# A graph layer on one Trainium2 core: the first norm of a joining group in six pieces, and a new order of passes in the FFN stream

## The chip, the core and the metric

The program runs on one core of one Trainium2 chip. The core has five engines that each follow their own list of instructions and meet only at semaphores: TensorE (PE in the profile, with its weight loads shown apart as PEld), VectorE (DVE), ScalarE (ACT), GpSimd (POOL) and SyncE (SP), which here only starts transfers. The metric is the device time of one execution in microseconds (us); lower is better.

## The reference, cut to what matters

A graph layer over 12500 nodes with 256 channels and 200000 edges sorted by destination:

```python
xn = layernorm(x)
support = xn @ gnn_weight                                  # 12500 x 256
agg = segment_sum(support[src] * edge_weight[:, None], dst, 12500)
x = x + relu(agg) + linear_attention(xn)                   # 4 heads of 64
h = layernorm(x)
for _ in range(30):                                        # the FFN
    h = h + 0.01 * tanh(h)
    h = h * sigmoid(h)
    h = layernorm(h, ln_w, ln_b)
    h = einsum("bsc,dc->bsd", h, W) + b
out = x + h
```

All is in float32. The 30 iterations on 12500 rows are the bulk of the work. A row never meets another row inside the FFN, so the rows can be worked in any order.

## The kernel before

**Tiling.** The 12500 nodes are 98 tiles of 128 rows. Four tiles make a group (G = 4), so there are 24 full groups and a last one of two tiles. One FFN iteration on one group is a *pass*; there are 25 x 30 = 750.

**Three stages.** First, x is loaded, normed and written out (`xnd`), the edge lists are transposed, and a part of the attention's key and value products is made. Second, the rest of these products, followed by the *mix chain*: a short row of dependent small matrices (`py`, `y`, `pbd`, `bd`, `pm`, `at`, `pm`, `mix`, lines 837 to 873) that folds the attention into one 256 x 256 matrix `mix`. Between its links the function `another_quad` is called twice. Third, the *FFN stream*, from about line 1025 to the end, in which all else is done step by step.

**The quads.** Edges are gathered 128 at a time: an indirect DMA issued by GpSimd (`gathers`, L196) brings the rows of `xnd` that belong to 128 edges into a tile `xg`, of which there are 16. Four of these make a *quad*: `selections` makes a matrix of weights on VectorE (L222, L227, L235), `sum_quad` multiplies on TensorE (L248, tile `pq`), ScalarE copies the sums of two quads (`copy_quads`, L259), and `add_quads` adds them by another matmul (L273) to a ring of nodes `pa`, which is copied out and cleared in `free_nodes` (L287, L288). There are 391 quads, about 16 to a group. Once a group's quads are done, its W matrix (aggregate times `wg`) can run, and with its mix matrix (`xnT` times `mix`) it makes the group's `base`, the x that goes into the FFN.

**The stream.** `plan()` writes out, before any instruction is issued, a list of steps. A step has at most one item: a pass, a mix matrix or a W matrix. It may also have a quad, a number of gathers, and the start of a group. `plan` keeps a clock of its own from fixed costs (T_PASS = 4.4 and so on) and takes a quad when the modelled landing of its gathers (T_LAND after the issue) lies in the past. At most ABREAST = 5 groups are in their 30 passes at a time, and two passes of one group are at least APART = 4 steps apart. Which of the ready groups gets the step is decided by

```python
if len(started) < len(groups) - 2 * ABREAST:
    g = min(ready, key=lambda g: (active[g][0], g))               # longest since its last pass
else:
    g = min(ready, key=lambda g: (active[g][1], active[g][0]))    # fewest passes done
```

A group starts ("joins") in the very step in which another one has left, if its base is there.

**A pass over several steps.** With its item in step k, a group is transposed on TensorE (L1001, tile `pt`) and copied by ScalarE (L1008, tile `zT`) in step k, multiplied by the FFN's matrix in k + 1 (L1014, tile `po`), and in k + 2 goes through tanh (ACT L960), the sum (DVE L966), silu (ACT L967), the statistics (DVE L973, `stats`) and their power of -1/2 on GpSimd (L977, L979). `normed` (DVE L987, tile `z`) follows one step later, and the group is ready to be transposed again. After its 30th pass, `po` is added to `base` into a tile `z` (L1075), and SyncE sends that to memory (L91). There are three `z` buffers, which `normed`, the outputs and the first norms share.

**A join before the change.** In step k, at its end: `ln_stats` with four bn_stats, four bn_aggr and a tensor_scalar on VectorE (L119, L121, L123) and a power on GpSimd (L125). In k + 1: the shift (L1097), four norms, half on VectorE (L1102) and half on ScalarE (L1107), and tanh. In k + 2: `act2`. In k + 3: `stats`. The group's first pass is planned for k + 5 or later.

Each engine works in the order in which the instructions were issued. GpSimd therefore does gathers and powers in one row, and a power that waits for VectorE holds back the gathers behind it.

Of the kernel before, what the change touches and what calls it, by code (L numbers as in the profile page):

```python
# [30 lines left out]
def gps_layer(  # L31
# [78 lines left out]
    nc.vector.memset(eps_t, EPS)  # L110
    root = first.tile([P, 1], F32, name="root")
    nc.scalar.activation(root, eps_t, AF.Sqrt)

    def ln_stats(pool, tl, nt, name):

        st = pool.tile([P, G, 6], F32, name=name + "_st")
        mv = pool.tile([P, G, 2], F32, name=name + "_mv")
        for j in range(nt):
            nc.vector.bn_stats(st[:, j, :], tl[:, j, :])  # L119
        for j in range(nt):  # L120
            nc.vector.bn_aggr(mv[:, j, :], st[:, j, :])  # L121
        ve = pool.tile([P, G], F32, name=name + "_ve")
        nc.vector.tensor_scalar(ve[:, :nt], mv[:, :nt, 1], 1.0, EPS, ALU.mult, ALU.add)  # L123
        rs = pool.tile([P, G], F32, name=name + "_rs")
        nc.gpsimd.tensor_tensor(rs[:, :nt], ve[:, :nt], mhalf[:, :nt], ALU.pow)  # L125
        return mv, rs

    def transposes_of(nat):

# [597 lines left out]
    with ExitStack() as ph:  # L727
# [112 lines left out]
        py = p_kv.tile([D + 1, HEADS, P], F32, name="pkv")  # L840
        for hd in range(HEADS):
            nc.tensor.matmul(py[:, hd, :], lhsT=psum_kv[:, hd, :], rhs=lk[:, hd % (P // D), :], start=True, stop=True)
        y = w1.tile([D + 1, HEADS, P], F32, name="y")
        nc.vector.tensor_copy(y, py)
        another_quad()
# [3 lines left out]
        for hd in range(HEADS):  # L849
            r = slice(hd % (P // D) * D, (hd % (P // D) + 1) * D)  # L850
            nc.vector.tensor_scalar(bd[r, hd // (P // D), r], pbd[r, hd, :], 1.0 / N, None, ALU.mult)


        at = w1.tile([P, KC, C], F32, name="at")
# [10 lines left out]
        for m in range(KC):  # L865
            for h in range(KC):
                nc.tensor.matmul(
                    pm[:, m, :], lhsT=at[:, h, m * P : (m + 1) * P], rhs=woT[:, h, :],
                    start=(h == 0), stop=(h == KC - 1),
                )  # L870
        nc.vector.scalar_tensor_tensor(
            mix, bo_r[:, None, :].to_broadcast([P, KC, C]), 1.0 / C, pm, op0=ALU.mult, op1=ALU.add
        )
# [6 lines left out]


    def plan():
        T_PASS, T_MATRIX, T_QUAD, T_GATHER, T_LAND, T_POW, T_STATS, T_CHAIN = 4.4, 3.5, 1.2, 1.25, 3.0, 1.3, 4.4, 14.0
        now, pool = 0.0, 4.0
        quads, got, started = ed.summed, ed.gathered, []
        whole, based = [], {}
        active, mixed, steps, k = {}, 0, [], 0
        landed = {t: 0.0 for t in range(got)}
        summed, passes = 0, 0
        pows = {}  # L890
        while len(based) < len(groups) or active or len(started) < len(groups):
            item, nq, cost, start = None, 0, 0.0, None
            octets = NO if quads == NQ else quads // 2
            while summed < len(groups) and octets > last_of[min((summed + 1) * G, NT) * P // SLOT - 1]:
                whole.append(summed)
                summed += 1
            ready = [g for g, (last, it, at) in active.items() if last + APART <= k and at <= now + 1.0]

            wanted = whole and mixed <= whole[0]
            if wanted or (not whole and not ready and mixed < len(groups)):  # L900
                item, cost = ("mix", mixed), T_MATRIX
                mixed += 1
            elif whole:
                item, cost = ("W", whole.pop(0)), T_MATRIX
                based[item[1]] = k
            elif ready:
                if len(started) < len(groups) - 2 * ABREAST:
                    g = min(ready, key=lambda g: (active[g][0], g))
                else:
                    g = min(ready, key=lambda g: (active[g][1], active[g][0]))  # L910
                it = active[g][1]
                passes += 1
                item, cost = ("pass", g, it), T_PASS
                if it == FFN_ITERS - 1:
                    del active[g]
                else:
                    active[g] = (k, it + 1, now + T_CHAIN)
                    pows[k + 2] = pows.get(k + 2, 0) + 1
            if len(active) < ABREAST and len(started) in based and based[len(started)] + 3 <= k:
                start = len(started)  # L920
                started.append(start)
                active[start] = (k + 1, 0, now + 18.0)
                pows[k] = pows.get(k, 0) + 1
                pows[k + 3] = pows.get(k + 3, 0) + 1

            ng, pool = 0, max(pool, now)
            while got < min(NE, quads * Q + ROWS) and pool < now + (T_STATS - T_GATHER if pows.get(k) else max(cost, 1.0)):
                pool += T_GATHER
                landed[got] = pool + T_LAND
                got += 1  # L930
                ng += 1
            if pows.get(k):
                pool = max(pool, now + T_STATS) + T_POW * pows[k]
            ahead = 2 * G * P / STEP * (ABREAST + 1.2 + passes / FFN_ITERS)
            while quads < min(NQ, ahead) and nq < (1 if item else 2):
                if max(landed.get(t, 1e9) for t in range(quads * Q, min(NE, (quads + 1) * Q))) > now + cost:
                    break
                quads += 1
                nq += 1
                cost += T_QUAD  # L940
            steps.append((item, nq, start, ng))
            now += max(cost, 1.0)
            k += 1
        return steps
# [77 lines left out]
    item = lambda k: steps[k][0] if 0 <= k < K and steps[k][0] else (None, None)  # L1022
    quads_of = lambda k: steps[k][1] if k < K else 0
    fresh = []
    selections(ed.summed + quads_of(0) - ed.selected)
    for k in range(K + 3):
        nq = quads_of(k)
# [40 lines left out]
            act2(g2, pos.pop((kind2, g2)), s2)  # L1068
        elif last:
            t0, nt = groups[g2]  # L1070
            o = fp.tile([P, G, C], F32, name="z", bufs=3)
            for q in range(nt // 2):
                h = pos[kind2, g2][:, q].rearrange("p c j -> p j c")
                r = slice(2 * q, 2 * q + 2)
                nc.vector.tensor_tensor(o[:, r, :], h, base[g2][:, r, :], ALU.add)  # L1075
            pos.pop((kind2, g2))
            rows_io(out, o, t0, nt, False, nc.sync)
        elif kind2 == "mix":
            nt = groups[g2][1]
            nc.vector.tensor_tensor(base[g2], pos.pop((kind2, g2))[:, :nt, :], xts.pop((kind2, g2))[:, :nt, :], ALU.add)  # L1080
        elif kind2 == "W":
            nt = groups[g2][1]
            ac = xts.pop((kind2, g2))[:, :nt, :]
            nc.vector.tensor_tensor(ac, pos.pop((kind2, g2))[:, :nt, :], ac, ALU.add)
            nc.vector.scalar_tensor_tensor(base[g2], ac, 0.0, base[g2], op0=ALU.max, op1=ALU.add)
        for d in (1, 2):
            kind3, g3 = item(k + d)[:2]
            if kind3 == "pass" and g3 in norm:
                normed(g3)

        for g3, k3 in list(fresh):
            if k == k3 + 1:
                nt = groups[g3][1]
                mv, rs = first_norm[g3]
                h = fp.tile([P, G // 2, C, 2], F32, name="z", bufs=3)
                sh = fp.tile([P, G], F32, name="f_ve")
                nc.vector.scalar_tensor_tensor(  # L1097
                    sh[:, :nt], mv[:, :nt, 0], -1.0, rs[:, :nt], op0=ALU.mult, op1=ALU.mult
                )
                for j in range(nt):  # L1100
                    if j % 2:
                        nc.vector.tensor_scalar(  # L1102
                            h[:, j // 2, :, j % 2], base[g3][:, j, :], mv[:, j, 0:1], rs[:, j : j + 1], ALU.subtract,
                            ALU.mult,
                        )
                    else:
                        nc.scalar.activation(  # L1107
                            h[:, j // 2, :, j % 2], base[g3][:, j, :], AF.Identity, bias=sh[:, j : j + 1],
                            scale=rs[:, j : j + 1],
                        )  # L1110
                first_norm[g3] = (h, act1(g3, h))
            elif k == k3 + 2:
                act2(g3, *first_norm[g3])
        if kind2 == "pass" and not last:
            stats(g2, s2)
        for g3, k3 in list(fresh):
            if k == k3 + 3:
                stats(g3, first_norm.pop(g3)[1])
                fresh.remove((g3, k3))
        start = steps[k][2] if k < K else None  # L1120
        if start is not None:
            first_norm[start] = ln_stats(fp, base[start], groups[start][1], "f")
            fresh.append((start, k))


# [29 lines left out]
```

## Time and profile before

| what | value |
|---|---|
| median of 3 runs | 4224.76 us (4222.74 to 4229.13) |
| the profiled execution: its time | 4296.01 us |
| the profiled execution: its span | 4294.2 us |
| TensorE busy | 4129.2 us, 96% of the span |
| weight loads busy | 3363.4 us, 78% |
| VectorE busy | 3392.1 us, 79% |
| ScalarE busy | 2541.6 us, 59% |
| GpSimd busy | 2589.4 us, 60% |
| FFN stream | from 433.6 us to the end |
| gathers in the span | 1563, 1018 ns mean |

The profiled execution is 71 us (1.7%) longer than the median of the unprofiled runs. All times of instructions below are from it. In the page's rows a group of instructions is given as line, engine, operation, tiles written and read, shapes, and then its busy time, the mean of one, and the idle time of its engine just before it with what ended that. "Busy" is the union of the intervals, and matmuls overlap each other, so that a matmul's mean (380 ns) is more than its share of the engine's time (2673.6 us over 11760, 227 ns).

### The profile page before, as it was taken

Reading aid. Unit: us, or ns where it says so; the run is one execution under the profiler, and the core shown is the slowest. Engines: PE = TensorE matmul, PEld = TensorE weight load, DVE = VectorE, ACT = ScalarE, POOL = GpSimd, SP = SyncE. Lnnn points to the kernel's source line nnn. Section 1 sums busy time; section 2 is a strip of 40 time slices with the busy share of each in tenths; the row PEclk is TensorE's granted clock in tenths of the full one; section 3 lists DMA queues with packets and bytes.
Section 4 is the critical chain, followed back from the end, with each engine's and each line's share of the span. In section 5 each row is a group of like instructions: output and inputs, shape, how many; then the busy total and the mean of one; then the engine's idle time right before and its main releaser. Section 6 shows DMA issues by size and latency. Waiting matters only on the chain.

```text
span 4294.2 us, 68066 instructions
## 1 busy us (share of the span) xinstructions
PE 4129.2 (96%) x24201; PEld 3363.4 (78%) x24201; DVE 3392.1 (79%) x7389; ACT 2541.6 (59%) x3762; POOL 2589.4 (60%) x3186
## 2 busy tenths in 40 slices
PE   8887999999989999999999999998999999999999
PEld 4444777888878878878788888886888888888888
DVE  8454678788778887778788887888888888988887
ACT  7322356556655656556566666665666667677776
POOL 3566777777767777777666666675666522222222
PEclk9998999999999999999999999999999999999999
DMA  8332422222222222222221212112212100000000
GB/s 255 105 88 85 139 85 68 73 74 68 70 73 74 70 86 69 80 79 62 77 68 53 80 56 62 56 57 88 66 57 65 47 4 1 25 1 1 1 1 22
DMA packets 147687, 278.35 MB, mean 65 GB/s; under 512 B 28048, under 2 KB 97198, under 8 KB 147342
## 3 DMA queue, kind: packets, MB, share of 16 engines
q0 software_dynamic: 75024, 204.97, 16.5%
q1 hardware_dynamic: 72173, 68.42, 5.2%
q8 instruction: 197, 3.23, 0.3%
q14 instruction: 149, 1.21, 0.1%
q10 hardware_dynamic: 144, 0.52, 0.0%
HBM read 247.68 MB, written 26.12 MB: 64 GB/s over the span
## 4 chain that ended last, share of the span: by engine, by line
PE 81%; DVE 8%; issue 3%; ACT 2%; POOL 2%; DMA 1%; another core or an unknown queue 0%; POOLq 0%; DVEq 0%; ACTq 0%
PE po L1014 54%; PE pt L1001 15%; PE pq L248 5%; PE pkv L302 3%; PE pa L273 3%; DVE z L987 2%; DVE st L973 2%; DVE s L966 2%; DMA xg<-xnd,src_i 1%; PE pacc L328 1%; ACT s L960 1%; ACT s L967 1%; POOL rs L979 1%; POOL xg L196 1%; DVE f_st L119 1%
## 5 line engine op out<-in xcount | busy, mean ns | idle before, releaser
L1014 PE MATMUL po<-w,zT 128*128 128x256 f32 x11760 | 2673.6, 380 | 1.8 <-issue 0.9
L1014 PEld LDWEIGHTS po<-w,zT 128*128 128x128 f32 x11760 | 2181.6, 191 | 281.7 <-issue 11.5
L196 POOL DMA_INDIRECT xg<-xnd,src_i x1563 | 1590.8, 1018 | 534.3 <-issue 357.3
L966 DVE SCALAR_TENSOR_TENSOR s<-s,po 128x1024 f32<-128x1024 f32 (+1 forms) x725 | 866.9, 1196 | 434.7 <-ACT s L960 387.0
L987 DVE TENSOR_SCALAR z<-s,st,rs 128x256 f32<-128x256 f32 x2940 | 1046.7, 419 | 107.8 <-POOL rs L979 76.4
L967 ACT ACTIVATE s<-s 128x1024 f32<-128x1024 f32 (+1 forms) x750 | 780.5, 1041 | 505.0 <-DVE s L966 466.1
L973 DVE BATCH_NORM_STATS2 st<-s 128x6 f32<-128x512 f32 x1470 | 938.6, 679 | 107.5 <-ACT s L967 98.3
L960 ACT ACTIVATE s<-po 128x1024 f32<-128x1024 f32 (+1 forms) x725 | 731.4, 1009 | 341.0 <-PE po L1014 309.2
L1008 ACT ACTIVATE zT<-pt 128x512 f32<-128x512 f32 x1470 | 800.8, 600 | 105.6 <-PE pt L1001 95.1
L1001 PEld LDWEIGHTS pt<-ident,z 128*128 128x128 f32 x5880 | 662.8, 142 | 227.0 <-issue 134.3
L1001 PE MATMUL pt<-ident,z 128*128 128x128 f32 x5880 | 795.6, 277 | 46.3 <-DVE z L987 27.3
L979 POOL TENSOR_TENSOR rs<-ve,mhalf 128x4 f32<-128x4 f32 (+1 forms) x750 | 777.1, 1036 | 62.4
L977 POOL TENSOR_SCALAR ve<-st 128x4 f32<-128x4 f32 (+1 forms) x750 | 153.9, 205 | 985.3 <-DVE st L973 954.9
L248 PE MATMUL pq<-xg,sel 128*32 128x256 f32 x3126 | 273.3, 394 | 37.7 <-DMA xg<-xnd,src_i 25.7
L259 ACT COPY sq<-pq 128x256 f32<-128x256 f32 x196 | 72.5, 370 | 333.7 <-PE pq L248 282.8
L287 ACT COPY aT<-pa 128x128 f32<-128x128 f32 x196 | 51.6, 264 | 268.1 <-PE pa L273 165.0
L302 PE MATMUL pkv<-wkv,big 128*128 128x512 f32 x392 | 200.7, 635 | 9.3 <-DVEq L636 4.9
L273 PE MATMUL pa<-selq,sq 128*128 128x192 f32 (+2 forms) x1168 | 184.4, 294 | 18.4 <-issue 9.4
L248 PEld LDWEIGHTS pq<-xg,sel 128*32 128x32 f32 x3126 | 67.8, 108 | 162.3 <-issue 112.7
L273 PEld LDWEIGHTS pa<-selq,sq 128*128 128x128 f32 x1168 | 171.0, 192 | 29.8 <-ACT sq L259 10.5
L313 DVE TENSOR_REDUCE v<-sq 128x8 f32<-128x512 f32 x98 | 67.0, 683 | 90.1 <-ACT sq L309 67.2
L302 PEld LDWEIGHTS pkv<-wkv,big 128*128 128x128 f32 x392 | 70.1, 198 | 79.4 <-issue 72.4
(146 smaller groups left out, 1513.4 us busy)
## 6 DMA issues: line engine op xcount, KB each, us to landing
xg<-xnd,src_i POOLq DMA_INDIRECT x1563
xt<-in_x_dram SPq DMA_DIRECT2D x48, 512.0 KB
xnd<-xt SPq DMA_DIRECT2D x24, 512.0 KB
xt<-accw SPq DMA_DIRECT2D x24, 512.0 KB
out_dram<-z SPq DMA_DIRECT2D x24, 512.0 KB
xg<-in_dst_dram SPq DMA_DIRECT2D x6, 128.0 KB
xg<-in_src_dram SPq DMA_DIRECT2D x6, 128.0 KB
xg<-in_edge_weight_dram SPq DMA_DIRECT2D x6, 128.0 KB
```

The costliest lines, as they stand in the source:

```text
L196: nc.gpsimd.indirect_dma_start(out=ed.xg[t], out_offset=None, in_=xnd, in_offset=bass.IndirectOffsetOnAxis(ap=src_i[:, t : t + 1], axis=0),)
L248: nc.tensor.matmul(ed.pq[j * 2 * WIN : (j + 1) * 2 * WIN, :], lhsT=sel[:, j, :], rhs=ed.xg.pop(q * Q + j), start=(q % 2 == 0), stop=last, ...
L273: nc.tensor.matmul(pa[:, k, c : c + hi - lo], lhsT=sq[:rows, k * P : (k + 1) * P], rhs=selq[:rows, lo - n0 : hi - n0], start=False, stop=( ...
L960: nc.scalar.activation(flat(s, nt), flat(h, nt), AF.Tanh)
L966: nc.vector.scalar_tensor_tensor(sf, sf, 0.01, flat(h, nt), op0=ALU.mult, op1=ALU.add)
L967: nc.scalar.activation(sf, sf, AF.Silu)
L973: nc.vector.bn_stats(st[:, q, :], s[:, q].rearrange("p c j -> p (c j)"))
L979: nc.gpsimd.tensor_tensor(rs[:, :nt], ve[:, :nt], mhalf[:, :nt], ALU.pow)
L987: nc.vector.tensor_scalar(z[:, j, :], s[:, j // 2, :, j % 2], sv[:, j, 1:2], rs[:, j : j + 1], ALU.subtract, ALU.mult)
L1001: nc.tensor.transpose(pt[:, i, k, :], z[:, 2 * q + i, k * P : (k + 1) * P], ident)
L1008: nc.scalar.activation(zT[:, 2 * q : 2 * q + 2], pt, AF.Copy, bias=1.0)
L1014: nc.tensor.matmul(po[:, j // 2, :, j % 2] if paired else po[:, j, :], lhsT=lhsT(j, k), rhs=rhs[:, k, :], start=(k == 0 and (j % 2 == 0 or ...
```

## The change

In the stream a join is spread over six steps. Step k: statistics of two of its four tiles. k + 1: statistics of the other two, bn_aggr, tensor_scalar and the power. k + 2: the shift and the norm of two tiles, one on ScalarE and one on VectorE. k + 3: the norm of the other two, and tanh. k + 4: `act2`, now ahead of the `normed` of that step. k + 5: `stats`. The group's first pass is planned no earlier than k + 7. The tile that takes the normed rows is group 0's `base`, once that group has been written out for two steps, and a `z` buffer before that.

An output is added into `base` itself and sent from there.

`plan` lets two joins be no less than four steps apart. Its choice of a pass goes by the passes done, counted on over fives of groups, and within a five each group is one pass behind the one before it until all groups have started; then this lag is dropped. T_LAND is 6.0 in place of 3.0, and the quads may run ahead of the passes by one group less. Powers and first passes are entered later, to fit the six steps.

In the mix chain, `another_quad` is called five times in place of two.

```diff
@@ mix chain
             nc.tensor.matmul(py[:, hd, :], lhsT=psum_kv[:, hd, :], rhs=lk[:, hd % (P // D), :], start=True, stop=True)
+        another_quad()
         y = w1.tile([D + 1, HEADS, P], F32, name="y")
         nc.vector.tensor_copy(y, py)
         another_quad()
...
             nc.vector.tensor_scalar(bd[r, hd // (P // D), r], pbd[r, hd, :], 1.0 / N, None, ALU.mult)
+        another_quad()
...
+        another_quad()
         nc.vector.scalar_tensor_tensor(
             mix, bo_r[:, None, :].to_broadcast([P, KC, C]), 1.0 / C, pm, op0=ALU.mult, op1=ALU.add
@@ plan
-        T_PASS, T_MATRIX, T_QUAD, T_GATHER, T_LAND, T_POW, T_STATS, T_CHAIN = 4.4, 3.5, 1.2, 1.25, 3.0, 1.3, 4.4, 14.0
+        T_PASS, T_MATRIX, T_QUAD, T_GATHER, T_LAND, T_POW, T_STATS, T_CHAIN = 4.4, 3.5, 1.2, 1.25, 6.0, 1.3, 4.4, 14.0
...
-                if len(started) < len(groups) - 2 * ABREAST:
-                    g = min(ready, key=lambda g: (active[g][0], g))
-                else:
-                    g = min(ready, key=lambda g: (active[g][1], active[g][0]))
+                lead = 0 if len(started) == len(groups) else 1
+                g = min(
+                    ready, key=lambda g: (
+                        active[g][1] + FFN_ITERS * (g // ABREAST) + lead * (g % ABREAST), active[g][0]
+                    ),
+                )
...
-            if len(active) < ABREAST and len(started) in based and based[len(started)] + 3 <= k:
+            if (
+                len(active) < ABREAST and len(started) in based and based[len(started)] + 3 <= k
+                and (not started or k >= started[-1] + 4)
+            ):
                 start = len(started)
-                started.append(start)
-                active[start] = (k + 1, 0, now + 18.0)
-                pows[k] = pows.get(k, 0) + 1
-                pows[k + 3] = pows.get(k + 3, 0) + 1
+                started.append(k)
+                active[start] = (k + 3, 0, now + 26.0)
+                pows[k + 1] = pows.get(k + 1, 0) + 1
+                pows[k + 5] = pows.get(k + 5, 0) + 1
...
-            ahead = 2 * G * P / STEP * (ABREAST + 1.2 + passes / FFN_ITERS)
+            ahead = 2 * G * P / STEP * (ABREAST + 0.2 + passes / FFN_ITERS)
@@ outputs
-            o = fp.tile([P, G, C], F32, name="z", bufs=3)
...
-                nc.vector.tensor_tensor(o[:, r, :], h, base[g2][:, r, :], ALU.add)
+                nc.vector.tensor_tensor(base[g2][:, r, :], h, base[g2][:, r, :], ALU.add)
             pos.pop((kind2, g2))
-            rows_io(out, o, t0, nt, False, nc.sync)
+            rows_io(out, base[g2], t0, nt, False, nc.sync)
+            written[g2] = k
@@ join, ahead of normed
+        for g3, k3 in fresh:
+            if k == k3 + 4:
+                act2(g3, *first_norm[g3])
@@ join, after normed
+            if k in (k3 + 2, k3 + 3):
+                mv, rs = first_norm[g3, "stats"]
+                if k == k3 + 2:
+                    if 0 in written and written[0] + 2 <= k:
+                        h = base[0].rearrange("p g c -> p (g c)").rearrange("p (q c j) -> p q c j", c=C, j=2)
                     else:
+                        h = fp.tile([P, G // 2, C, 2], F32, name="z", bufs=3)
...
+                q = k - k3 - 2
+                if 2 * q < nt:
+                    nc.scalar.activation(
+                        h[:, q, :, 0], base[g3][:, 2 * q, :], AF.Identity, bias=sh[:, 2 * q : 2 * q + 1],
+                        scale=rs[:, 2 * q : 2 * q + 1],
+                    )
+                    nc.vector.tensor_scalar(
+                        h[:, q, :, 1], base[g3][:, 2 * q + 1, :], mv[:, 2 * q + 1, 0:1], rs[:, 2 * q + 1 : 2 * q + 2],
+                        ALU.subtract, ALU.mult,
+                    )
+                if k == k3 + 3:
+                    first_norm[g3] = (h, act1(g3, h))
@@ join, at the end of the step
+            for j in range(nt):
+                if j // 2 == k - k3:
+                    nc.vector.bn_stats(first_norm[g3, "st"][:, j, :], base[g3][:, j, :])
+            if k == k3 + 1:
...
+                nc.gpsimd.tensor_tensor(rs[:, :nt], ve[:, :nt], mhalf[:, :nt], ALU.pow)
+                first_norm[g3, "stats"] = (mv, rs)
+            elif k == k3 + 5:
+                stats(g3, first_norm[g3][1])
```

More of the change, by code (lines that the diff above doesn't have):

```diff
@@ L112, in gps_layer @@
     nc.scalar.activation(root, eps_t, AF.Sqrt)
[L114 to L126, printed above, removed]
     def transposes_of(nat):
@@ L1024, in gps_layer @@
     fresh = []
+    written = {}
     selections(ed.summed + quads_of(0) - ed.selected)
@@ L1089, in gps_layer @@
                 normed(g3)
[L1091 to L1105, printed above, removed]
-                    else:
[L1107 to L1113, printed above, removed]
+        for g3, k3 in fresh:
+            nt = groups[g3][1]
+            if k in (k3 + 2, k3 + 3):
[3 more added lines that the diff above has]
+                        h = base[0].rearrange("p g c -> p (g c)").rearrange("p (q c j) -> p q c j", c=C, j=2)
+                    else:
+                        h = fp.tile([P, G // 2, C, 2], F32, name="z", bufs=3)
+                    sh = fp.tile([P, G], F32, name="f_ve")
+                    nc.vector.scalar_tensor_tensor(
+                        sh[:, :nt], mv[:, :nt, 0], -1.0, rs[:, :nt], op0=ALU.mult, op1=ALU.mult
+                    )
+                    first_norm[g3, "h"] = (h, sh)
+                h, sh = first_norm[g3, "h"]
+                q = k - k3 - 2
[7 more added lines that the diff above has]
+                        ALU.subtract, ALU.mult,
+                    )
+                if k == k3 + 3:
+                    first_norm[g3] = (h, act1(g3, h))
@@ L1114, in gps_layer @@
         if kind2 == "pass" and not last:
             stats(g2, s2)
[L1116 to L1119, printed above, removed]
         start = steps[k][2] if k < K else None
         if start is not None:
-            first_norm[start] = ln_stats(fp, base[start], groups[start][1], "f")
             fresh.append((start, k))
+        for g3, k3 in list(fresh):
+            nt = groups[g3][1]
+            if k == k3:
+                first_norm[g3, "st"] = fp.tile([P, G, 6], F32, name="f_st")
+            for j in range(nt):
+                if j // 2 == k - k3:
+                    nc.vector.bn_stats(first_norm[g3, "st"][:, j, :], base[g3][:, j, :])
+            if k == k3 + 1:
+                mv = fp.tile([P, G, 2], F32, name="f_mv")
+                for j in range(nt):
+                    nc.vector.bn_aggr(mv[:, j, :], first_norm[g3, "st"][:, j, :])
+                ve = fp.tile([P, G], F32, name="f_ve")
+                nc.vector.tensor_scalar(ve[:, :nt], mv[:, :nt, 1], 1.0, EPS, ALU.mult, ALU.add)
+                rs = fp.tile([P, G], F32, name="f_rs")
+                nc.gpsimd.tensor_tensor(rs[:, :nt], ve[:, :nt], mhalf[:, :nt], ALU.pow)
+                first_norm[g3, "stats"] = (mv, rs)
+            elif k == k3 + 5:
+                stats(g3, first_norm[g3][1])
+                fresh.remove((g3, k3))
```

## The prediction

> **What bounds the kernel now.** I read the busy times on the page first.
>
> ```profile
> span 4294.2 us, 68066 instructions
> ...
> PE 4129.2 (96%) x24201; PEld 3363.4 (78%) x24201; DVE 3392.1 (79%) x7389; ACT 2541.6 (59%) x3762; POOL 2589.4 (60%) x3186
> ```
>
> TensorE is the bound. Of its 165 us of idle time about 86 lie ahead of the stream, which begins at 433.6 us, and all but the mix chain there is left as it is. So the question is what the stream loses. The busy times by stretch, for the four stretches that hold most joins and one without joins or quads:
>
> ```profile
> core 0: us, PE busy (x) PEld busy (x) DVE busy (x) ACT busy (x) POOL busy (x), PEclk, DMA share, GB/s
> 1190.00:1300.00 110.00, 96.53 (x551) 77.73 (x550) 85.58 (x203) 58.65 (x87) 69.92 (x81) 0.95 0.24 72
> 2040.00:2110.00 70.00, 60.62 (x351) 48.33 (x351) 54.59 (x127) 39.30 (x58) 41.90 (x50) 0.98 0.29 85
> 2890.00:3010.00 120.00, 105.99 (x605) 85.37 (x604) 99.07 (x234) 64.48 (x96) 68.14 (x83) 0.99 0.28 84
> 3670.00:3730.00 60.00, 54.84 (x276) 46.17 (x275) 56.82 (x141) 38.38 (x56) 18.39 (x29) 0.94 0.13 45
> 4000.00:4100.00 100.00, 100.00 (x554) 89.12 (x553) 86.39 (x165) 70.48 (x98) 29.75 (x52) 1.00 0.00 1
> ```
>
> Without joins TensorE is never idle and a full pass takes 4.33 us (from one start of transposes to the next). In the join stretches it is idle for 42 of 360 us. The Trainium skill (Perfetto Trace Analysis, Identifying the Most-Contended Engine) calls matmul busy time a bad measure of headroom and would have me read the weight loads' share, 78% overall against 89% in the steady stretch: a tenth or more open. But the change removes no matmul and alters none. A pass at 100% busy stays at 4.33 us, so I count idle time and half clock only; by the page's rule the ceiling would be hundreds of us.
>
> Who ends TensorE's waits, over the whole span:
>
> ```profile
> PE pt L1001 <- DVE z L987: 27.3, 25, 3.8
> PE pq L248 <- DMA xg<-xnd,src_i: 25.7, 18, 4.6
> PE pt L1001 <- ACT zT L1008: 14.4, 11, 2.5
> ```
>
> From the timeline I listed the gaps of TensorE in the stream: 79 us. 25.5 of them wait for gathered rows; 41.5 are waits for norms or copies within some steps of a join; 12 are scattered (1.0 ahead of the first mix matrix, 2.2 at the last W matrix, and the like).
>
> How a join costs, on VectorE in the row of five (3680 to 3707 us):
>
> ```profile
> 3689.90 1.22 DVE L966 SCALAR_TENSOR_TENSOR s<-s,z 128x1024 f32<-128x1024 f32 x1
> 3691.03 0.15 DVE L1097 SCALAR_TENSOR_TENSOR f_ve<-f_mv,f_rs 128x4 f32<-128x4 f32 x1
> 3691.12 0.74 DVE L1102 TENSOR_SCALAR z<-big,f_mv,f_rs 128x256 f32<-128x256 f32 x2
> 3691.77 1.28 DVE L973 BATCH_NORM_STATS2 st<-s 128x6 f32<-128x512 f32 x2
> 3692.97 1.39 DVE L119 BATCH_NORM_STATS2 f_st<-big 128x6 f32<-128x256 f32 x4
> 3694.27 0.36 DVE L121 BATCH_NORM_AGGREGATE f_mv<-f_st 128x2 f32<-128x6 f32 x4
> 3694.67 0.17 DVE L123 TENSOR_SCALAR f_ve<-f_mv 128x4 f32<-128x4 f32 x1
> ```
>
> VectorE runs without a break: parts of three different joins lie in one step, and only then come the output's adds and the norm that TensorE waits for. Four starts of transposes, 3682.56 to 3709.41, took 26.85 us instead of 17.3: 9.5 us lost.
>
> And how a join starves a quad:
>
> ```profile
> 1217.04 1.03 POOL L125 TENSOR_TENSOR f_rs<-f_ve,mhalf 128x4 f32<-128x4 f32 x1 [5.63 <-DVE f_ve L123]
> ...
> 1221.12 1.06 PE L248 MATMUL pq<-xg,sel 128*32 128x256 f32 x2 [4.64 <-DMA xg<-xnd,src_i]
> ```
>
> GpSimd stood 5.6 us at the first norm's power, with gathers behind it. The next gather was issued at 1218.27 and used at 1221.12, 2.85 us later.
>
> **The clock.** The granted clock is 0.5 in eight stretches of 3.4 us in the stream (one pair of them adjacent); TensorE was busy in 25.4 us of these, which costs half, 12.7 us: 4.4 after DMA gaps, 8.3 after join gaps. TensorE: Matmul & The Clock Gate in the Trainium skill (Why this matters for your kernels) asks for no idle gap over about 3 us. Here a gap of 2.13 us was punished and one of 2.25 was not (the first row is the stretch after the one, the second that after the other):
>
> ```profile
> 830.70:834.10 3.40, 3.40 (x13) 3.08 (x13) 1.98 (x4) 3.11 (x5) 2.50 (x3) 0.50 0.32 90
> 955.30:958.70 3.40, 3.40 (x19) 2.78 (x20) 1.41 (x2) 2.44 (x5) 2.49 (x4) 1.00 0.39 108
> ```
>
> By the rule only the three gaps over 3 us (4.64, 3.78, 3.30) cost clock, about 6 us, and the sum below would be some 6 us smaller. I take the trace's 12.7.
>
> **The change part by part.**
>
> *Order of steps.* Worked out from them, the planner's rules give 800 steps before and after, none without an item. Quads in the stream: 344, then 341. Joins before: 4, 6, 8, 28, 53; 149 to 210; 307 to 371; 483 to 495; 645 to 649, one a step. After: 4, 8, 12, 23, 47; 159 to 182; 314 to 336; 473 to 497; 635 to 656, four to seven apart. TensorE's work is the same, so only gaps can change.
>
> *Joins.* On VectorE one takes 1.39 + 0.36 + 0.17 + 0.15 + 0.74 + 1.22 + 1.28 = 5.3 us; the leaving group's last pass saves 1.22 + 1.28 and adds 1.28 for its output, so net 4.1. Spread over six steps the most that it adds to one is 1.28; two overlapping joins add up to 2.5. With quads, VectorE has 0.9 us spare per step (2500 to 3000: 409 busy of 500 in about 100 steps), 4.5 in five: that covers 4.1. Without quads it has 4.33 - 3.88 = 0.45. The last five joins (635 to 661; the last quad is in step 623) bring 20.5 against 26 x 0.45 = 11.7; a norm is made up to one step (4.3 us) ahead of its use, so about 4.5 us are lost, not 9.5. For the other twenty I take 0.5 us each, between nothing and the 1.1 to 2.2 that a join by itself costs now (gaps at 1551, 2199, 2371): 10. Half clock, two stretches: 3. Together 17.5, against 49.7 now (41.5 + 8.2): **-32**. Bounds: -45 and -5.
>
> What queues where: `act2` of a join (1.22) now stands ahead of the `normed` of its step, and transposes of that pass wait for it where the group comes round in four steps; by five the norm has a step to spare, which hides it. ScalarE gets the same instructions (59% busy). GpSimd has the same 25 powers of 1.0 us.
>
> *T_LAND.* The planner leaves 3 us more between a gather and its quad. All DMA gaps but one are 2.3 us or less, and the one of 4.64 came from the power above. I keep a fifth of 29.9 (25.5 + 4.4): **-24**. Bounds: -30, and -8 if lateness of GpSimd, not the margin, makes most of them. Taking quads later could starve a W matrix, but no step is empty and no start slips by more than 15 steps.
>
> *Outputs in place.* The adds are the same (0.68 each). VectorE's 5.9 us of waiting for output transfers go (3.5 in `normed`, 2.4 in L1075), inside the join stretches, so counted already. SyncE sends the same transfers in the same order. The first norm's writes to group 0's base wait for its output, six steps old at first use: nothing.
>
> *Mix chain.* From 410 to 434 us TensorE is busy 12.7 of 24, at half clock, and waits 5.2 for `y` and 5.0 for `bd`. Three quads more (about 1.1 + 1.2 each there) fit into these waits, but the last stands before the first mix matrix, and VectorE's selections (0.8) ahead of `y`. I take 2 us longer for 3 x 1.3 fewer in the stream: **-2**. Bounds -6 and +5, the latter if the rows of the fourth and fifth quad (1.25 us of GpSimd each) aren't there.
>
> *Sum.* -32 - 24 - 2 = -58, made against the profiled 4296.0: 4238. The median is 71 us under that; gaps hardly scale, so 4224.8 - 58 = **4167**.
>
> **The rivals.**
>
> *Overload only smeared (0.23).* Passes four steps apart have about 1.5 us between norm and use instead of a step more, and there are 104 of them (90 before), 25 in steps 650 to 700 where no quad gives VectorE time. Joins then gain 8, T_LAND 14, the chain nothing: 4203. For: VectorE's 4.67 us per step against TensorE's 4.33 in the last five joins. Against: the other twenty have quads beside them.
>
> *Late norms at four apart (0.06), slower.* About 60 of these passes lie in steps of joins. If each waits 2 us for its norm (two joins overlapping add 1.9 to 2.5), that is 120, less the 50 of now, less 26 for T_LAND and the chain: +44, 4269. It decides from 1.3 us per pass on. Against: such waits are rarer than four-step passes before (25 waits for z).
>
> *Nothing gained (0.07).* The gaps are passed on: a wait of TensorE for VectorE turns into one for a copy or for a gather, and the planner's clock meets the engines no better than before: 4224.
>
> *Main case (0.64):* 4167, itself 4145 to 4195.
>
> **Numbers.** A measurement of this kernel can tell about 0.2% (8.4 us) from no change. Faster: 0.64 + 0.23 = 0.87; same 0.07; slower 0.06. The range 4143 to 4208 takes in the main case and most of the smeared one.
>
> **What would show it.** Right: starts of the first norm four or more steps apart; TensorE's wait for gathered rows at 5 us instead of 25.7; its wait for z below 12; 3 half-clock stretches or fewer in the stream; TensorE's idle time in the stream near 30 us with the same 4.33 per pass; span near 4236. Wrong: VectorE at 95% through 26 steps of the last joins with gaps of 1 to 2 us in each; waits for gathers as before; a chain of mix much over 24 us.

## The result, and the profile after

The changed kernel takes 4167.57 us (median of 4 runs, 4166.53 to 4168.22), the one before 4224.38: ratio 0.9863, interval 0.9851 to 0.9875, 56.8 us faster. The forecast was 4167.

One thing has to be said first, or the two profiles can't be compared. The program's time depends on the chip. In what follows, chip C is the one on which the kernel before takes 4224 us, A the one with 4286, B the one with 4300. The profile of before, with its 4296 us, looks like A and B, not like C: it spends the time in the second stage. The profile after comes from C. Busy time by stage (second stage, mix chain, stream; columns as before), first of before:

```profile
core 0: us, PE busy (x) PEld busy (x) DVE busy (x) ACT busy (x) POOL busy (x), PEclk, DMA share, GB/s
138.00:401.00 263.00, 221.42 (x1316) 117.17 (x1314) 134.46 (x347) 72.17 (x183) 164.60 (x174) 0.97 0.30 88
401.00:433.60 32.60, 17.97 (x102) 11.21 (x100) 10.93 (x34) 2.74 (x8) 17.68 (x19) 0.63 0.25 73
433.60:4294.00 3860.40, 3777.55 (x22202) 3169.68 (x22202) 3142.44 (x6613) 2371.15 (x3368) 2354.07 (x2886) 1.00 0.20 57
```

and of the changed kernel:

```profile
139.00:345.00 206.00, 205.76 (x1317) 113.00 (x1316) 136.98 (x352) 72.43 (x183) 156.02 (x165) 1.00 0.37 106
345.00:384.50 39.50, 26.92 (x143) 13.09 (x141) 12.56 (x44) 3.45 (x10) 30.05 (x32) 0.97 0.43 130
384.50:4166.00 3781.50, 3749.26 (x22163) 3152.84 (x22162) 3142.85 (x6595) 2371.39 (x3364) 2348.71 (x2882) 1.00 0.20 58
```

The second stage has the same instructions in both and takes 57 us more in the first; that is the chip (the changed kernel itself needs 55 us more on B than on C up to the end of this stage, as the table below shows). What the change did is in the other two rows: the stream is 79 us shorter in this pair, and the chain, measured from the last product of the second stage (tile `pacc`) to the first mix matrix, is 35.7 us instead of 28.0. Part of these differences is the chip's, too, since the runs on one chip differ by 57 us only.

The head of the page after:

```profile
span 4166.0 us, 67989 instructions
...
PE 4095.5 (98%) x24201; PEld 3346.7 (80%) x24201; DVE 3397.5 (82%) x7389; ACT 2544.1 (61%) x3762; POOL 2588.0 (62%) x3186
```

Four stretches of the changed kernel with most of the joins, and the steady one:

```profile
core 0: us, PE busy (x) PEld busy (x) DVE busy (x) ACT busy (x) POOL busy (x), PEclk, DMA share, GB/s
1195.00:1300.00 105.00, 101.16 (x591) 82.37 (x590) 94.24 (x217) 65.30 (x96) 71.07 (x85) 1.00 0.24 72
2000.00:2090.00 90.00, 86.15 (x506) 70.69 (x505) 80.90 (x188) 55.46 (x82) 59.41 (x71) 0.98 0.26 78
2775.00:2870.00 95.00, 92.02 (x542) 74.84 (x541) 85.25 (x199) 59.33 (x87) 62.33 (x73) 1.00 0.26 77
3510.00:3660.00 150.00, 140.58 (x752) 120.66 (x751) 130.82 (x275) 99.91 (x137) 42.72 (x70) 0.99 0.04 15
4000.00:4100.00 100.00, 100.00 (x556) 89.22 (x555) 86.60 (x164) 70.82 (x98) 29.75 (x52) 1.00 0.00 1
```

TensorE is idle for 20.1 us in 440 us of these join stretches; it was 42 in 360. In the last stretch, without quads, VectorE is busy 87% of the time and TensorE still loses 9.4 us. Its waits over the whole span:

```profile
PE pt L996 <- DVE z L982: 20.3, 25, 2.4
PE pq L234 <- DMA xg<-xnd,src_i: 13.8, 19, 1.9
```

Of the 13.8 us for gathered rows, 2.1 lie in the stream; the rest is in the mix chain and at the end of the second stage. All idle time of TensorE in the stream is 27.9 us (79 before), and half clock is granted in two stretches of it (2017 and 3591 us) and at its two ends.

### The profile page after: what moved, and what is told of

Same layout as the page of the kernel before. It is cut to its first block, busy times and chain, and to the rows that moved or that the text cites. A ratio compares the mean times of both kernels' runs of the same rounds, so it can differ in the third digit from the quotient of the medians.

```text
span 4166.0 us, 67989 instructions
## 1 busy us (share of the span) xinstructions
PE 4095.5 (98%) x24201; PEld 3346.7 (80%) x24201; DVE 3397.5 (82%) x7389; ACT 2544.1 (61%) x3762; POOL 2588.0 (62%) x3186
## 4 chain that ended last, share of the span: by engine, by line
PE 81%; DVE 10%; ACT 2%; issue 1%; POOL 1%; DMA 1%; POOLq 0%; ACTq 0%; DVEq 0%
PE po L1009 55%; PE pt L996 14%; PE pq L234 5%; DVE z L982 3%; PE pkv L288 3%; PE pa L259 3%; DVE st L968 2%; DVE s L961 2%; ACT s L955 2%; DMA xg<-xnd,src_i 1%; PE pacc L314 1%; POOL rs L974 1%; DVE f_st L1131 1%; DVE big L1070 0%; ACT s L962 0%
## 5 line engine op out<-in xcount | busy, mean ns | idle before, releaser
L996 PE MATMUL pt<-ident,z 128*128 128x128 f32 x5880 | 793.0, 276 | 20.9 <-DVE z L982 20.3
L234 PE MATMUL pq<-xg,sel 128*32 128x256 f32 x3126 | 264.6, 392 | 13.8 <-DMA xg<-xnd,src_i 13.8
L295 ACT ACTIVATE sq<-pkv 128x512 f32<-128x512 f32 x98 | 58.2, 593 | 102.5 <-PE pkv L288 102.5
```

The source lines that it names most:

```text
L234: nc.tensor.matmul(ed.pq[j * 2 * WIN : (j + 1) * 2 * WIN, :], lhsT=sel[:, j, :], rhs=ed.xg.pop(q * Q + j), start=(q % 2 == 0), stop=last, ...
L996: nc.tensor.transpose(pt[:, i, k, :], z[:, 2 * q + i, k * P : (k + 1) * P], ident)
```

## The experiments

The chip matters as much as the edit, so runs are compared on one chip only. Lengths of stages in the profiles, in us (to the last `pacc`; from there to the first mix matrix; from there to the end):

| kernel | chip | to `pacc` | chain | stream | median of runs | before on that chip |
|---|---|---|---|---|---|---|
| before, second profile | A | 401.8 | 24.5 | 3857.9 | 4285.9 | 4285.8 |
| before, T_LAND 6 | A | 404.6 | 24.3 | 3807.7 | 4234.2 | 4285.8 |
| before, T_LAND 6 | B | 405.4 | 27.6 | 3810.2 | 4244.5 | 4299.6 |
| changed, T_LAND 3 | A | 401.6 | 38.8 | 3814.3 | 4259.5 | 4285.8 |
| changed, T_LAND 3 | B | 404.2 | 39.5 | 3825.6 | 4269.4 | 4299.6 |
| changed | B | 404.6 | 39.4 | 3800.7 | 4245.2 | 4299.6 |
| changed | C | 349.3 | 35.5 | 3781.6 | 4166.3 | 4224.5 |
| changed, two calls | A | 401.6 | 24.0 | 3796.5 | 4224.0 | 4285.8 |
| changed, two calls, longer lag | B | 407.2 | 27.9 | 3796.0 | 4232.1 | 4299.6 |

**The kernel before, a second profile** (no edit).

> The kernel before, once more, for a second profile. As predicted (theory A: the lost time is 25 us of late gathers and 41 us at joins): the stream loses the same as in the first profile, TensorE waits about 25 us for gathered rows and about 41 us around joins, and the second stage (138 to 401 us) is 263 us long again. Rival (theory B: the first profile, 71 us over the median, shows waits that the timed runs don't have): the second stage takes about 206 us as it does in the changed kernel's profile, TensorE's waits for gathered rows in the stream are under 12 us, the waits around joins stay near 41 to 50, and the span is near 4224.

4285.94 us, on a chip where before takes 4285.75. Theory B falls as it was put: the second stage takes 258 us again, and the waits in the stream are those of the first profile.

```profile
PE pt L1001 <- DVE z L987: 28.3, 26, 3.8
PE pq L248 <- DMA xg<-xnd,src_i: 24.6, 17, 4.6
PE pt L1001 <- ACT zT L1008: 16.1, 13, 2.5
```

So these waits are no accident of one execution; a chip of this kind has them each time. On C no profile of the kernel before was taken, and how much of them it has there stays open.

**T_LAND alone**, on A, then on B.

```diff
-        ... = 4.4, 3.5, 1.2, 1.25, 3.0, 1.3, 4.4, 14.0
+        ... = 4.4, 3.5, 1.2, 1.25, 6.0, 1.3, 4.4, 14.0
```

> The kernel before with T_LAND 6.0 in the planner in place of 3.0, and nothing else. A: 24 us faster, 4200. B: the waits for gathers are small in an undisturbed run, so 0 to 6 us faster, 4218 to 4224. A third outcome, slower by up to 8, if quads taken later crowd W matrices into the joins.

> The kernel before with T_LAND 6 alone, again, because the kernel before takes 4286 us on one chip and 4224 on another. Theory C (late gathers are the larger part on every chip): 40 to 52 us faster than before on this chip too. Theory D (late gathers weigh that much only where the second stage also stands still): 15 to 30 us.

On A 4234.20 us, ratio 0.9878 (0.9863 to 0.9893), 51.6 faster; on B 4244.53, ratio 0.9872 (0.9857 to 0.9887), 55.1 faster. One constant in the planner gives, on these chips, as much as the whole change, twice what I had put down for it and more than any of the theories expected. TensorE's waits with T_LAND 6, on A:

```profile
PE pt L1001 <- ACT zT L1008: 20.0, 14, 2.7
PE pt L1001 <- DVE z L987: 19.9, 21, 2.9
...
PE pq L248 <- DMA xg<-xnd,src_i: 1.6, 2, 1.1
```

The waits for rows are gone and those for norms and copies are hardly less (39.9 us against 44.4). The stream is 50 us shorter, though, and the waits for rows were 24. The rest is in the quads' own row of the page, first in the second profile of the kernel before, then with T_LAND 6, both on A (busy time and mean; then idle time before):

```profile
L248 PE MATMUL pq<-xg,sel 128*32 128x256 f32 x3126 | 271.8, 393 | 32.3 <-DMA xg<-xnd,src_i 24.6
```

```profile
L248 PE MATMUL pq<-xg,sel 128*32 128x256 f32 x3126 | 257.3, 393 | 9.6 <-issue 4.9
```

The same matmuls, of the same mean length, keep TensorE "busy" 14.5 us less (16 in the stream). A quad that came too early for its rows shows why (second profile of the kernel before):

```profile
819.50 0.63 PE L248 MATMUL pq<-xg,sel 128*32 128x256 f32 x6
822.28 0.62 PE L248 MATMUL pq<-xg,sel 128*32 128x256 f32 x2 [2.15 <-DMA xg<-xnd,src_i]
```

The eight matmuls of a quad overlap and take 0.64 us together when nothing holds them up (the median). Here the first six take 0.63, and the last two, which waited for the fourth gather, take 0.62 again by themselves. So a late gather costs its gap and about 0.6 us more, and these 0.6 us count as busy. In this trace 22 of the stream's 342 quads begin before the last of their rows has landed. They hold 24.7 us of gaps and 14.7 us of busy time beyond the median. With T_LAND 6 one quad does. The list of gaps had missed this part of the cost. Transposes give another 5 us, half clock 1.

**The changed kernel with T_LAND back at 3.0**, on A, then on B (the same edit reversed).

> The changed kernel with T_LAND back at 3.0. A: 24 us slower than the changed kernel, 4191. B: 0 to 6 us slower, 4168 to 4174.

> The changed kernel with T_LAND 3, again beside it. C: 30 to 36 us slower than the changed kernel. As predicted: 24. D: 8 to 15.

On A 4259.52 us, ratio 0.9937 (0.9923 to 0.9950): the rest of the change is worth 26 us without T_LAND. On B 4269.39, ratio 0.9930 (0.9917 to 0.9944), 30.2 below before and 24.2 above the changed kernel. Waits for gathered rows are 11.9 us on A (24.6 in the kernel before), so the rest of the change halves them. That the joins lie apart doesn't explain it: in the kernel before only 3 of the 22 late quads fall within 12 us of the statistics of a first norm. With the rest of the change no quad after 1081 us is late on A; that fits the edit by which quads may run ahead by one group less (`ahead`), but no run has that edit alone.

**The changed kernel itself**, on C, then on B (no edit).

> The changed kernel itself, beside the others, so that the margin, the joins and the chain can be set against each other on one chip. T_LAND alone took 51 us off, the rest of the change without T_LAND 26, the changed kernel with two calls in the chain 62. Theory C (late gathers are the larger part, and joins overlap with it): 55 to 63 us faster than before. If the chain's three quads cost what their stage shows (36 us against 24), it is 6 to 10 us behind the one with two calls; if the stream gives that back, within 3.

> The changed kernel, to stand beside the three below on one chip. 57 to 61 us faster than before. With the kernel before, before with T_LAND 6 and the changed kernel with T_LAND 3 it makes a square: if the two effects simply added up, it would be the sum of the two beside it (77 us on the chip where both were measured); if both remove the same stalls, less.

On C 4166.31 us, ratio 0.9858 (0.9842 to 0.9875), 58.2 faster; on B 4245.20, ratio 0.9868 (0.9853 to 0.9884), 54.4 faster, a little less than expected there. B now has all four kernels, with and without each of the two parts (the "square"): T_LAND alone -55.1, the rest alone -30.2, both -54.4. Put on first, T_LAND brings 55; put on last, 24. The rest brings 30 first and nothing last.

**Two calls of another_quad in the chain**, on A, and with the longer lag on B.

```diff
             nc.tensor.matmul(py[:, hd, :], lhsT=psum_kv[:, hd, :], rhs=lk[:, hd % (P // D), :], start=True, stop=True)
-        another_quad()
...
             nc.vector.tensor_scalar(bd[r, hd // (P // D), r], pbd[r, hd, :], 1.0 / N, None, ALU.mult)
-        another_quad()
...
-        another_quad()
         nc.vector.scalar_tensor_tensor(
...
-                lead = 0 if len(started) == len(groups) else 1
+                lead = 0 if len(started) == len(groups) and passes >= 680 else 1
```

The last edit is in the run on B alone.

> The changed kernel with the mix chain's three added calls of another_quad taken out (two calls are left). A (the three quads save 2 us in all): 4169 to 4170. Rival (its profile shows the chain at 35.7 us from the last key-value product to the first mix matrix, with GpSimd's gathers back to back and TensorE waiting 1.2 us for each pair of rows): the chain shrinks by 10 to 14 us, the stream gains three quads of 1.3 us, so 6 to 10 us faster, 4157 to 4162. Third: the gathers only move into the stream's start, which is then bound by GpSimd, and the time stays within 3 us.

> The changed kernel with the lag kept until 680 passes are done (1 us faster by itself, within its spread) and two calls of another_quad in the mix chain instead of five. If the 36 us chain is paid in full, 6 to 12 us faster than the changed kernel; if the stream's start is bound by GpSimd's gathers, as its five quads are, within 3 us of it. If the quads in the chain help: 2 to 4 us slower.

On A 4224.01 us, ratio 0.9856 (0.9841 to 0.9871); the changed kernel was not run on A, so this says only that it does no worse than the change does elsewhere. On B 4232.09, ratio 0.9842 (0.9828 to 0.9855), 13.1 below the changed kernel, of which the lag by itself is about 1 (below). It is the fastest version on B; on C it was not run. The chain, with five calls and with two, on B:

```profile
404.60:444.00 39.40, 21.87 (x113) 13.12 (x111) 9.91 (x37) 2.55 (x8) 25.67 (x28) 0.57 0.34 91
```

```profile
407.20:435.10 27.90, 15.06 (x73) 9.50 (x70) 7.07 (x22) 1.28 (x4) 14.86 (x17) 0.57 0.25 74
```

The chain is 11.5 us shorter with two calls, while the stream, which then has three quads more, is 4.7 shorter as well. Why five calls take so long differs by chip. On C, where two calls were not run, GpSimd is the bound of this stage. TensorE there:

```profile
353.31 1.09 PE L828 MATMUL pkv<-lk,psum_kv 65*65 65x128 f32 x8
354.33 0.62 PE L234 MATMUL pq<-xg,sel 128*32 128x256 f32 x2
355.28 0.62 PE L234 MATMUL pq<-xg,sel 128*32 128x256 f32 x2 [0.33 <-DMA xg<-xnd,src_i]
356.54 0.62 PE L234 MATMUL pq<-xg,sel 128*32 128x256 f32 x2 [0.64 <-DMA xg<-xnd,src_i]
357.92 0.62 PE L234 MATMUL pq<-xg,sel 128*32 128x256 f32 x2 [0.76 <-DMA xg<-xnd,src_i]
359.05 0.92 PE L259 MATMUL pa<-selq,sq 128*128 128x192 f32 x4 [0.52 <-ACT sq L245]
```

and GpSimd in the same time:

```profile
353.71 0.95 POOL L182 DMA_INDIRECT xg<-xnd,src_i  x1 [0.30 <-PE pq L234]
354.96 1.12 POOL L182 DMA_INDIRECT xg<-xnd,src_i  x1 [0.30 <-PE pq L234]
356.38 0.95 POOL L182 DMA_INDIRECT xg<-xnd,src_i  x1 [0.30 <-issue]
357.63 0.95 POOL L182 DMA_INDIRECT xg<-xnd,src_i  x1 [0.30 <-issue]
```

A gather takes 0.95 us and the next starts 0.30 later, 5 us for a quad. The quad put between `py` and `pbd` waits for its rows pair by pair, and the next link of the chain stands behind it in TensorE's order. At this stage no rows are in store on C: 29 gathers at 1.25 us are 36 us, the whole chain.

On B, where the 11.5 us were measured, this is not what happens. The rows of the chain's quads had landed 7 to 17 us before the quads began, and TensorE waits for no rows in this stage; A shows the same. Some of the longest waits of ScalarE and TensorE in the chain with five calls on B (404.6 to 444 us):

```profile
ACT sq L245 <- remote: 16.2, 2, 13.4
PE pa L259 <- issue: 6.4, 1, 6.4
PE pa L259 <- ACT sq L245: 4.9, 3, 2.9
```

ScalarE stands for up to 13.4 us ahead of a copy of the quads' sums, and "remote" is a releaser that the profile doesn't know. So on A and B the cost of the three calls is shown, and its cause is not.

**The join in four steps again**, on C.

```diff
-            if k == k3 + 4:
+            elif k == k3 + 2:
                 act2(g3, *first_norm[g3])
...
-            if k in (k3 + 2, k3 + 3):
-                mv, rs = first_norm[g3, "stats"]
+            if k == k3 + 1:
+                nt = groups[g3][1]
+                mv, rs = first_norm[g3]
+                h = fp.tile([P, G // 2, C, 2], F32, name="z", bufs=3)
...
-            elif k == k3 + 5:
-                stats(g3, first_norm[g3][1])
+            if k == k3 + 3:
+                stats(g3, first_norm.pop(g3)[1])
...
+            first_norm[start] = ln_stats(fp, base[start], groups[start][1], "f")
```

> The changed kernel with the first norm in four steps as before (bn_stats of four tiles and the aggregates in step k, four norms in k + 1, act2 in k + 2, stats in k + 3); order of passes, distance of joins, T_LAND, outputs and chain as changed. As predicted (a join by itself cost 1.1 to 2.2 us in the old form, 0.5 in the new): 10 to 25 us slower than the changed kernel. Rival (the distance between joins does it all, VectorE's sum is the same): within 4 us of it.

The edit also puts the first norm's rows back into a `z` buffer, `act2` behind `normed`, and the powers at their old steps in the plan.

4174.03 us, ratio 0.9877 (0.9860 to 0.9893), 7.7 slower than the changed kernel, between the two expectations. The distance and order of joins and T_LAND keep most of the gain; splitting the first norm is the smaller part, and some of the 7.7 may be the buffer's (below). TensorE's waits:

```profile
PE pt L1010 <- DVE z L996: 16.8, 26, 1.3
...
PE pt L1010 <- ACT zT L1017: 6.8, 10, 1.1
```

The waits for norms are as many as in the changed kernel and shorter; waits for ScalarE's copies `zT`, of which the six-step join leaves 0.3 us, come back, and 3.6 us of the waits fall on passes five steps apart, which have none in the changed kernel.

**Outputs and first norms in z buffers again**, on C.

```diff
-                nc.vector.tensor_tensor(base[g2][:, r, :], h, base[g2][:, r, :], ALU.add)
+                nc.vector.tensor_tensor(o[:, r, :], h, base[g2][:, r, :], ALU.add)
...
-                    if 0 in written and written[0] + 2 <= k:
+                    if False:
```

> The changed kernel with outputs added into a z buffer and the first norm's rows in a z buffer, as before. As predicted (nothing, beyond 5.9 us of waits for output transfers that the old kernel had within its joins): 0 to 3 us slower. Rival (three z buffers shared by norms, outputs in transfer and first norms hold back the norms at every join): 8 to 20 us slower.

4169.04 us (4167.88 to 4171.11) against 4166.31 (4165.55 to 4168.24): 2.7 slower, within what was predicted and hardly more than the spread of the runs.

**The lag kept longer**, on C (the edit shown above, with five calls in the chain).

> The changed kernel with the lag of one pass between the groups of a five kept until 680 passes are done, and dropped then: the catching up at four steps apart moves from steps 661 to 699, next to the last joins, to 730 to 769, away from them. If the stalls of the last join stretch (9 us of TensorE's idle time and 1.7 us of half clock between 3510 and 3660) come from norms that are late at four steps apart: 4 to 8 us faster. If from VectorE's overload by the last five joins alone: the same, within 2. If four steps apart stall without joins too: the stalls move along with them, the same or slower.

4165.12 us (4162.26 to 4167.32), ratio 0.9857 (0.9840 to 0.9873): 1.2 below the changed kernel, not beyond its spread. The stalls at 3545, 3565, 3575 and 3587 us are as in the changed kernel; two later ones (1.4 and 0.3 us) are gone, and the passes at four steps apart that now come at 730 to 769 cost 1.1 us in all. So these cost little without joins beside them. Joins alone don't stall TensorE either. Setting the trace of the changed kernel against the planner's steps, 18.1 of the 20.6 us of waits ahead of transposes fall on passes that come four steps after the group's last one (16.0 on the 58 of them that lie within seven steps of the start of a join, 2.1 on the other 46), and 2.5 on first passes. The 511 passes at five steps apart have none, though 49 of them lie beside a join. This run left 15 passes at four steps apart at 640 to 663, and all four stalls fall on such passes. In these traces it takes both, a join and a pass four steps apart; a plan that keeps five steps while groups join was not tried. The first stall, in the changed kernel:

```profile
3543.24 1.06 ACT L955 ACTIVATE s<-big 128x1024 f32<-128x1024 f32 x1
3544.20 1.00 ACT L955 ACTIVATE s<-po 128x1024 f32<-128x1024 f32 x1
...
3545.24 1.22 DVE L961 SCALAR_TENSOR_TENSOR s<-s,po 128x1024 f32<-128x1024 f32 x1 [1.23 <-ACT s L955]
3546.38 1.22 DVE L961 SCALAR_TENSOR_TENSOR s<-s,big 128x1024 f32<-128x1024 f32 x1
...
3547.51 1.38 DVE L982 TENSOR_SCALAR z<-s,st,rs 128x256 f32<-128x256 f32 x4
...
3548.06 1.21 PE L996 MATMUL pt<-ident,z 128*128 128x128 f32 x7 [2.45 <-DVE z L982]
```

This stall isn't VectorE's load: VectorE itself waits 1.23 us for ScalarE, where a join's tanh stands ahead of the pass's. Then comes a join's `act2`, ahead of the norm that TensorE needs.

## Why the prediction was right, point by point

The sum was right, on C to the microsecond and on B to 4 us. Its terms were not all right: the chain's is 14 us off, with the wrong sign, and the joins' about 10 us the other way (estimate below). That it came out to the microsecond is luck.

- *T_LAND, -24.* As the last thing put on it measures 24.2 (B). Alone it is 51.6 and 55.1. The term was sized from gaps of TensorE, and the step that failed is "TensorE's work is the same, so only gaps can change": some 15 us of the cost of late rows were inside the quads' busy time. The Trainium skill's warning against matmul busy time (Perfetto Trace Analysis, Identifying the Most-Contended Engine), which I had weighed for the 96% as a whole and set aside, gives pipelining as its reason. The row of quads agrees: the same pipelined matmuls count as 257.3 us busy in unbroken rows and as 271.8 where gaps break them. A gather's rows are there 2.5 us after its start by the packets in the traces (median, on every chip) and within 3.6 us in 95 of 100. Of the 22 late quads, 13 are late by GpSimd's turn alone: their last gather started less than 3.0 us ahead of the quad and landed within 3.0 us. In the other 9 the landing itself took longer than the planner's 3.0 us, up to 5.4, and 8 of these had started late as well.
- *Joins, -32.* With T_LAND at 3 on A, the stream loses 43.6 us, about 4 of them for three quads fewer: -40 for order, distance and form of the joins and for `ahead`, with half of the late gathers in it. With T_LAND at 6 on B only 9.5 us come out of the stream, although waits for norms and copies fell from 41 to 23: the start of the stream gave most of it back. In its first 150 us TensorE is idle for 14 us (5 with T_LAND alone), and the mix matrices take 6.5 us longer in that profile. The five calls are not the main cause: with two, TensorE is still idle for 12.6 us there and the mix matrices take 5.0 us longer. On C the idle time there is 3 us. The cause stays open.
- *The residue.* I left 17.5 us at the joins; waits of 23 and 4 of half clock are left on C. The cause in the text, VectorE's overload in the last five joins, is at most part of it: VectorE is at 87%, and the stall shown starts at ScalarE, which I had passed over with "the same instructions (59% busy)". In that stall order counted, not load. The remark that a join's work is hidden at five steps apart and not at four was right: all waits ahead of transposes but those of first passes lie at four. That the place of `act2` makes them is not shown: with `act2` behind `normed` and the join in four steps, such passes beside joins still wait 15.6 us.
- *Mix chain, -2, bounds -6 and +5.* Wrong in sign and beyond its bound: the chain is 12 to 14 us longer in the traces of A and B, and taking the three calls out gains 12 (13.1 less about 1 for the lag). I had seen TensorE's 10 us of waiting and filled it. These waits were VectorE's: it stood for 7.2 us ahead of `y` and 5.9 ahead of `bd`, by a releaser that the profile doesn't know (`DVE y L844 <- remote: 7.2, 1, 7.2`). The missing rows, which I had named for the upper bound, were missing on C, and there for all quads of the chain instead of two; on A and B they were there, and the cost came by waits of ScalarE and VectorE that are not explained.
- *Outputs in place, nothing.* 2.7 us, within its 0 to 3.
- *The rivals.* The smeared overload did not come: 4203 would have been outside. Late norms at four apart came, but small: 16.0 us on 58 passes beside joins, 0.3 us each where the rival takes 2. Nothing gained is excluded by every interval above.
- *What was to be seen.* Right: first norms four or more steps apart, idle time near 30 us (27.9), at most three stretches of half clock in the stream, 4.33 us per pass. Wrong: waits for z below 12 (20.3); waits for gathered rows at 5 (13.8, though 2.1 in the stream); the span of 4236, which took the chip of the first profile for granted (4166 on C, 4244.7 on B). Of the signs of being wrong one came, a chain much over 24 us (35.7).

So by the square on B the change is worth 54 us in two ways of counting: -30 for all the rest and -24 for T_LAND, close to the prediction's -34 and -24, or -55 for T_LAND and nothing for the rest. The prediction's split was one of several that the same runs allow. Split three ways, with the chain apart, it would be near -42, +12 and -24; this is an estimate, since the calls were taken out with T_LAND at 6 only.

## What to carry to other kernels

Two edits that keep the same engine from waiting don't add up: price each both as the first and as the last one put on. A gap in a row of short, overlapping matmuls costs more than its length, and the rest counts as busy time; so hold a row's busy time against that of a version or a stretch without gaps. Before filling an engine's idle time with other work, ask what keeps it idle and which engine feeds the filler: one that waits for its own data, as on C, stands ahead of the chain that it was to hide in.

## What the runs showed of the hardware that was not expected

The same second stage, with the same instructions, took 206 us on one chip, TensorE busy for all of it, and 258 to 265 us on two others (TensorE busy 225 to 226), the whole program 1.4 to 1.8% more; the landing time of gathers was the same on all. In the mix chain of these two ScalarE and VectorE stand for up to 13 us. What stands still was not found: the traces put part of it down to releasers that they don't know.
